# Attention logits: four float32 row tiles of 32 channels instead of stacks of float32r halves

## The chip, the cores and the metric

The kernel runs on one core of one Trainium2 chip. The metric is the device time of one execution in microseconds (us); lower is better. The kernel before takes 4385.15 us, the median of three runs (4384.52 to 4387.54).

## What is computed

Two layers on an image batch x of shape (2, 256, 64, 64), all in float32. A "position" is one of the 4096 pixels of an image.

```python
# layer 0: group norm, then a Mamba block over 4096 positions, residual added
x = x + _L0_conv_ref(_gn(x), ...)
# layer 1: group norm, then attention with 8 heads of 32 channels, residual added
qkv = jnp.einsum('bchw,oc->bohw', x, qkv_w) + qkv_b[None, :, None, None]
q, k, v = ...                                  # (2, 8 heads, 32 channels, 4096)
attn_logits = jnp.einsum('bhci,bhcj->bhij', q, k) * scale
attn_weights = jax.nn.softmax(attn_logits, axis=-1)
out = jnp.einsum('bhij,bhcj->bhci', attn_weights, v)
x = x + out
```

## The kernel before

The program has two stages, one after the other on the same core.

**Mamba stage** (`mamba_stage`, L263). Each image is cut into 8 tiles of 512 positions, 16 tiles in all. One tile's work is 32 steps of the recurrence plus projections before (`front`), gates (`gate`) and the feed-forward part after (`back`). Every operation is handed to a planner with `add(engine, due, cost, emit, reads, writes)`; `Plan.order` (L185) then writes out one fixed order of instructions per engine. It takes, whenever an engine is free in its own bookkeeping, the ready task with the smallest due time, adds `SWITCH` to a task that needs another activation table, and refuses tasks more than `HORIZON` ahead of the oldest one. So the due times, not the program text, set the order in the queues. While image 1 is in this stage, `qkv` (L715) also computes queries, keys and values of image 0: TensorE projects, ScalarE writes the rounded high half in float32r (`high`, L751), VectorE writes the remainder (`low`, L755), and both halves go to DRAM (L760).

**Attention stage** (`attention`, L969). Heads are taken in groups of four (128 channels). A query tile has 512 positions, so there are 2 images x 2 groups x 8 = 32 query tiles. For each, a loop runs over 32 key blocks of 128 positions; one turn of it is called a step here, and there are 1024. A step s does, in the order in which `run` (L1261) issues it:

- `exponentials(s, 0)` and `(s, 1)`: ScalarE reads the logits of two heads (128 x 1024) from PSUM and writes their exponentials to SBUF. The first pair of heads goes into a `chunk` (a tile that collects several terms), the second into a tile `e`.
- `values(s - 1)`: four TensorE matmuls, one per head, 32 output columns each, so that they occupy four column tiles of the array at once. They add into `po`.
- `logits(s + 1, 0)` and `(s + 1, 1)`: two matmuls each. The logits land in tiles `s` of two PSUM banks, of which there are three (`ps_s`, bufs=3). The tiles are used in turn, so the second half of one step takes over the tile that the first half of the step before has filled, and has to wait until that exponential has been read out.
- `add_up(s)`: the softmax denominators. VectorE sums a full chunk with one TENSOR_REDUCE (L1183) and puts the sum as first term into the next chunk. GpSimd and VectorE add up the second pair of heads.

At the start of the next query tile `finish` (L1226) copies `po` out of PSUM (L1232, on VectorE) before the next tile's first `values` may write there, since `po` has one buffer. Later, four more matmuls sum over the partitions (L1242), and reciprocal, scaling and residual follow.

A logit matmul before is one float32r matmul over 128 rows: for each head the rows hold the 32 channels four times, as high and low halves of keys against high and low halves of queries. `load_stack` (L954) builds these stacks from DRAM: a 512-position query tile is read by four DMAs, a key tile of one group by two. Keys of the second group replace those of the first while its last query tile runs (L1271). Between the images `prepare` (L1076) computes image 1's queries, keys and values on the spot (`project`, L1040, `project_values`, L1062): halves go out to DRAM through chunk tiles and the keys come back as stacks.

A chunk before holds four terms, so at steps c = 3, 6, 9, ... 30 of each query tile a reduce of 4 x 1024 elements per partition runs, ten per tile. The last (c = 30) writes `acc_sb`.

Of the kernel before, what the change touches and what calls it, by code (L numbers as in the profile page):

```python
# [23 lines left out]
D = 32  # L24
# [231 lines left out]
SWITCH = 10  # L256
HORIZON = 28
# [5 lines left out]
def mamba_stage(ctx, tc, xs, stats_out, consts, w, outs, scratch):  # L263
# [70 lines left out]
    def first(b, t, due):  # L334
        xt = Buf(r_h)
        load = lambda: nc.sync.dma_start(xt.tile, image_tile(xs[b], t))
        stats = lambda k: nc.vector.bn_stats(stats_in[b][:, k, t, :], xt.tile[:, k, :])
        if b == 0:

            xt.tile = r_h.make()  # L340
            load()
            for k in range(KC):
                stats(k)
            return
        add("SP", due + 8, 0.8, load, [], [xt], lands=3.0)
        for k in range(KC):
            add("DVE", due + 1.5, 0.7, lambda k=k: stats(k), [xt], [stats_bufs[b][k * NT + t]])
# [102 lines left out]
    def group_norm(b, k, due):  # L450
# [27 lines left out]
        add("PE", due, 0.4, lambda: matmul(p1.tile[:, 0:1], [(gmat, s.tile[:, 0:1])]), [s], [p1])  # L478
        add("DVE", due + 1, 0.6, spread, [p1], [s])
        add("PE", due - 1.5, 0.4, lambda: matmul(p2.tile[:, 0:1], [(gmat, s.tile[:, 4:5])]), [s], [p2])  # L480
        add("ACT", due, 0.6, root, [p2], [s, out], ("exp",))
        add("DVE", due - 7.5, 0.2, shift, [s], [out])
# [10 lines left out]
    def front(i):  # L493
# [10 lines left out]
        if i:  # L504
            add("SP", due - 43.5, 1.7, lambda: nc.sync.dma_start(yn.tile, image_tile(xs[b], t)), [], [yn], lands=3.3)
        for k in range(KC):
            add("ACT", due - 31, 0.72, lambda k=k: norm(k), [yn[k], scales_buf[b * KC + k]], [yn[k]])
# [3 lines left out]
        add("PE", due - 40, 1.72, lambda: matmul(mean.tile, [(lnmat, yn.tile[:, k, :]) for k in range(KC)]), [yn], [mean])  # L511
        sq = [Buf(r_tmp) for _ in range(KC)]
        var = Buf(mm)
        for k in range(KC):
# [4 lines left out]
            add("DVE", due - 40.5, 0.6, centre, [mean], [yn[k]])  # L519
            square = lambda k=k: nc.scalar.activation(sq[k].tile, yn.tile[:, k, :], AF.Square)  # L520
            add("ACT", due - 32.5, 0.52, square, [yn[k]], [sq[k], var] if k == 0 else [sq[k]])
# [6 lines left out]
        add("PE", due - 41.5, 1.72, lambda: matmul(var.tile, [(lnmat, s.tile) for s in sq]), sq, [var])  # L528
        add("ACT", due - 36.5, 1.19, rstd, [], [var], ("exp",))
        for k in range(KC):  # L530
# [9 lines left out]
            add("DVE", due - 45, 0.66, scale, [var], [yn[k]])  # L540
            add("ACT", due - 35.5, 0.62, shift, [], [yn[k]])
# [19 lines left out]
        add("PE", due - 11, 3.44, project, d.u, [pp, proj, bc])  # L561
        add("ACT", due - 3, 0.48, lambda: nc.scalar.copy(proj.tile[:NP, :], pp.tile[:NP, :]), [pp], [proj])
        add("ACT", due - 13.5, 0.48, lambda: nc.scalar.copy(bc.tile, pp.tile[:NP, :]), [pp], [bc])
        add("SP", due - 14, 0.4, store_bc, [bc], [d.bc], lands=1.6)
        add("DVE", due - 16, 0.72, halves, [pp, proj], [proj])
# [4 lines left out]
    def conv(d, b, k, due):  # L570
# [13 lines left out]
        add("PE", due - 10, 1.72, project, [d.yn], [px, xm])  # L584
        add("ACT", due - 5, 0.15, lambda: nc.scalar.copy(xm.tile[:, 0:HALO], halo[:, b, k, :]), [h], [xm[0]])
        add("ACT", due + 2, 0.49, lambda: nc.scalar.copy(xm.tile[:, HALO:], px.tile), [px], [xm[1]])
        add("ACT", due + 4, 0.25, lambda: nc.scalar.copy(halo[:, b, k, :], xm.tile[:, T:]), [xm], [h])
        add("PE", due + 4.5, 3.44, convolve, [xm], [pc, d.u[k]])
        add("ACT", due + 0.5, 0.59, silu, [pc], [d.u[k]], ("silu",))

    def softplus(d, k, due):
# [22 lines left out]
        add("PE", due - 3.5, 0.5, lambda: matmul(pd.tile, [(w_dt[:, i, bass.ts(k, P)], d.proj.tile) for i in range(2)]), [d.proj], [pd, dt, lw])  # L614
        add("ACT", due - 2, 1.76, exps, [], [pd, dt], ("exp",))
        add("ACT", due + 2.5, 0.97, logs, [pd], [lw, w1], ("exp",))
        add("DVE", due - 3, 0.58, rest, [pd], [w1])
        add("POOL", due + 7, 1.23, lambda: nc.gpsimd.tensor_sub(lw.tile, lw.tile, w1.tile), [w1], [lw])
        add("POOL", due + 5.5, 1.23, lambda: nc.gpsimd.tensor_add(dt.tile, dt.tile, lw.tile), [lw], [dt])
        add("SP", due + 9, 0.9, lambda: store(d.dt[k], dt, "dt_dram"), [dt], [d.dt[k]], lands=2.0)  # L620
        add("POOL", due - 0.5, 1.23, lambda: nc.gpsimd.tensor_mul(lw.tile, dt.tile, d.u[k].tile), [dt, d.u[k]], [lw])
        add("SP", due + 9.5, 0.9, lambda: store(d.dtu[k], lw, "dtu_dram"), [lw], [d.dtu[k]], lands=2.0)

    def gate(d, k, due):
# [7 lines left out]
        add("PE", due + 7.5, 1.72, project, [d.yn], [pz, z])  # L632
        add("ACT", due + 9, 0.5, lambda: nc.scalar.activation(z.tile, pz.tile, AF.Silu), [pz], [z], ("silu",))

    def back(i):
# [5 lines left out]
        for m in range(KC):  # L641
# [13 lines left out]
            for k in range(0, KD, 2):  # L655
                reads = [yn[m], *d.z] if k == 0 else d.z[k : k + 2]
                work = 2.58 if k == 0 and b == 0 else 1.72
                add("PE", due + 2 * m - 3.5, work, lambda k=k, project=project: (project(k), project(k + 1)), reads, [po])
# [3 lines left out]
            else:  # L662
                plus = lambda m=m, po=po: nc.vector.tensor_add(yn.tile[:, m, :], yn.tile[:, m, :], po.tile)
                add("DVE", due + 2 * m - 1.5, 0.6, plus, [po], [yn[m]])
        hid = Buf(r_hid, KH)
        xt = Buf(r_xb, KC)
        add("SP", due + 5, 1.7, lambda: nc.sync.dma_start(xt.tile, image_tile(xs[b], t)), [], [xt], lands=3.3)
        for f in range(KH):
# [8 lines left out]
            add("PE", due + 5 + 1.5 * f + 0.5, 1.72, up, [yn], [ph, hid if f == 0 else hid[f]])  # L677
            add("ACT", due + 6 + 1.5 * f - 6.5, 0.59, gelu, [ph], [hid[f]], ("gelu",))
        for m in range(KC):
# [12 lines left out]
            for f in range(0, KH, 2):  # L692
                reads = [hid, yn[m], *([xt[m]] if b == 0 else [])] if f == 0 else [hid[f], hid[f + 1]]
                work = 1.72 if f else 3.44 if b == 0 else 2.58
                add("PE", due + 19 + 4 * m + f / 2, work, lambda f=f, down=down: down(f), reads, [acc])
# [11 lines left out]
            if b == 0:  # L707
                add("ACT", due + 24 + 4 * m + 4, 0.59, end, [acc], [xt[m]])
            else:
                add("DVE", due + 24 + 4 * m - 3, 0.76, end, [acc], [xt[m]])  # L710
            add("DVE", due + 25 + 4 * m - 0.5, 0.61, stats, [xt[m]], [stats_bufs[IMAGES + b][m * NT + t]])
        store = lambda: nc.sync.dma_start(image_tile(outs[b], t), xt.tile)
        add("SP", due + 29.5, 1.7, store, [xt], [stored[b * NT + t]], lands=3.3)

    def qkv(b, t, due):  # L715

        hid = Buf(r_hid, KH)
        halves = [hid[5], hid[6]]

# [17 lines left out]
        add("SP", due + 4, 1.7, load, [stored[b * NT + t]], [hid], lands=3.3)  # L737
        for c in range(KC):
            w_parts = [hid[0]] if c == 0 else [hid[1], hid[2]]
            add("SP", due + 1 + c + 7, 1.3, lambda c=c: load_weights(c), [], w_parts, lands=3.0)  # L740
        for k in range(KC):
            add("ACT", due + 3.5, 0.71, lambda k=k: norm(k), [hid[3 + k], scales_buf[(IMAGES + b) * KC + k]], [hid[3 + k]])
        for n, (i, m) in enumerate(((1, 0), (1, 1), (0, 0), (0, 1))):
# [5 lines left out]
            def high(i=i, m=m, pm=pm):  # L749
                bias = b_qkv[:, i * KC + m : i * KC + m + 1]  # L750
                nc.scalar.activation(hid.tile[:, 5, :].bitcast(F32R), pm.tile, AF.Identity, bias=bias)  # L751

            def low(i=i, m=m, pm=pm):
                bias = b_qkv[:, i * KC + m : i * KC + m + 1]
                nc.vector.scalar_tensor_tensor(  # L755
                    hid.tile[:, 6, :].bitcast(F32R), pm.tile, bias, hid.tile[:, 5, :], ALU.add, ALU.subtract
                )

            def store(i=i, m=m):
                nc.sync.dma_start(  # L760
# [730 lines left out]
```

## Time and profile before

The profiled execution took 4385.95 us; its span on the core is 4384.2 us, so 1.75 us lie around the span, and it stands 0.8 us above the median of the runs.

| stretch of the trace | from to (us) | what |
|---|---|---|
| Mamba stage | 0 to 1996 | 16 tiles; 115 to 116 us each for image 0, 117 us each for image 1 |
| attention, image 0 | 1996 to 3137 | 16 query tiles of 70.8 us |
| prepare | 3137 to 3232 | projections of image 1 |
| attention, image 1 | 3232 to 4384 | 16 query tiles of 70.8 us and the end |

The page gives for each engine its busy time, for groups of instructions the number, the mean duration and the idle time before them with its releaser. A matmul's record covers the whole pipeline, so records of TensorE overlap; the distance between the starts of two is the time that one takes of the array. A float32 matmul appears as two records of 512 columns (start to start 0.43 us each where nothing else is in the way, e.g. at L688), a float32r matmul as one.

### The profile page before, as it was taken

What the parts mean: (1) busy time and instruction counts of PE and PEld (TensorE: products, weight loads), DVE (VectorE), ACT (ScalarE), POOL (GpSimd) and SP (SyncE); (2) the same over time, 40 slices, a digit from 0 to 9 for tenths busy, and PEclk for the clock granted to TensorE, in tenths of its full rate; (3) what the DMA queues carried; (4) which work ended last, traced back from release to release, by engine and by line L of the source; (5) the groups of instructions that cost most, each with busy time, mean ns of one, the idle gap of its engine ahead of it and who ended that gap; (6) DMA issues with size and microseconds to landing.
All of it is one profiled execution on the core that took longest, in us unless ns stands there. A gap on an engine that the chain in (4) does not pass through costs nothing.

```text
span 4384.2 us, 53753 instructions
## 1 busy us (share of the span) xinstructions
PE 4208.9 (96%) x18594; PEld 1644.3 (38%) x18594; DVE 3879.8 (88%) x3309; ACT 3765.4 (86%) x4982; POOL 3726.1 (85%) x1913
## 2 busy tenths in 40 slices
PE   6799999999999999989999999999999999999998
PEld 2233333333333433333333333333443333333333
DVE  5899999999999999985888888888758888888898
ACT  5788988988888888767999999999669999999997
POOL 3999999999999999985888888888548888888886
PEclk8899999999999999999999999999999999999999
DMA  6333333333444444436010221010362010410100
GB/s 210 108 109 126 129 117 118 118 125 125 161 166 154 158 157 151 149 115 148 17 27 18 51 70 27 18 27 20 100 196 56 27 27 24 100 27 18 27 20 9
DMA packets 172281, 389.24 MB, mean 89 GB/s; under 512 B 23392, under 2 KB 49760, under 8 KB 163808
## 3 DMA queue, kind: packets, MB, share of 16 engines
q1 hardware_dynamic: 171120, 383.37, 28.5%
q10 hardware_dynamic: 880, 2.36, 0.2%
q8 instruction: 148, 2.42, 0.2%
q14 instruction: 133, 1.09, 0.1%
HBM read 292.33 MB, written 93.32 MB: 88 GB/s over the span
## 4 chain that ended last, share of the span: by engine, by line
PE 80%; DVE 10%; ACT 4%; issue 2%; DMA 2%; POOL 1%; SPq 0%; DVEq 0%; POOLq 0%; ACTq 0%
PE s L1161 26%; PE po L1191 24%; PE mm L448 14%; DVE h L869 6%; PE mm L688 4%; PE y L901 4%; PE bn L448 2%; PE mm L647 2%; DVE bn L860 1%; ACT L248 1%; ACT da L853 1%; PE s L1046 1%; PE y L899 1%; PE sums_ps L1242 1%; DMA dtu_dram<-lw 1%
## 5 line engine op out<-in xcount | busy, mean ns | idle before, releaser
L1183 DVE TENSOR_REDUCE chunk<-chunk 128x1024 f32<-128x4096 f32 x288 | 1270.6, 4412 | 242.2 <-ACT chunk L1174 242.1
L1224 POOL TENSOR_TENSOR acc_p<-acc_p,e 128x1024 f32<-128x1024 f32 x480 | 1151.8, 2400 | 196.8 <-ACT e L1174 178.4
L1174 ACT ACTIVATE chunk<-s 128x1024 f32<-128x1024 f32 x992 | 1121.2, 1130 | 185.7 <-PE s L1161 144.1
L1161 PE MATMUL s<-q,k 128*128 128x512 f32 x4096 | 1227.2, 421 | 7.3 <-ACT chunk L1174 6.4
L875 POOL TENSOR_TENSOR h<-h,c 128x1024 f32<-128x1024 f32 x512 | 1202.7, 2373 | 29.3 <-issue 13.3
L1191 PE MATMUL po<-chunk,v 128*32 128x512 f32 x3968 | 1121.2, 642 | 0.0
L1191 PE MATMUL po<-e,v 128*32 128x512 f32 x4224 | 1079.2, 605 | 0.0
L1174 ACT ACTIVATE e<-s 128x1024 f32<-128x1024 f32 x1056 | 1071.9, 1018 | 7.6 <-PE s L1161 7.2
L1161 PEld LDWEIGHTS s<-q,k 128*128 128x128 f32 x4096 | 690.5, 188 | 1015.6 <-issue 914.8
L853 ACT ACTIVATE da<-dt_rep,neg_a 128x512 f32<-128x512 f32 x1024 | 695.8, 702 | 106.5 <-DVE h L869 103.6
L1222 POOL TENSOR_TENSOR acc_p<-acc_p,e 128x512 f32<-128x512 f32 x480 | 620.4, 1293 | 129.2 <-ACT e L1174 106.6
L869 DVE TENSOR_TENSOR_SCAN h<-da,state,dbu 128x512 f32<-128x512 f32 x512 | 650.8, 1274 | 15.7 <-PE y L901 7.4
L869 DVE TENSOR_TENSOR_SCAN h<-da,state,bn 128x512 f32<-128x512 f32 x512 | 646.3, 1262 | 11.1 <-PE y L901 5.4
L864 POOL TENSOR_TENSOR dbu<-dtu_rep,b 128x1024 f32<-128x1024 f32 x176 | 417.3, 2371 | 19.8 <-issue 7.7
L448 PE MATMUL bn<-proj,pick 112*128 112x512 f32 x512 | 342.7, 671 | 85.6 <-DVE h L869 82.6
L248 ACT ACT_TABLE_LOAD x312 | 400.3, 1283 | 6.3 <-PEq L1481 0.7
L860 DVE TENSOR_TENSOR bn<-dtu_rep,bn 128x512 f32<-128x512 f32 x512 | 346.1, 678 | 18.0 <-DMA dtu_rep<-dtu_dram 9.2
L1221 DVE TENSOR_TENSOR acc<-acc,e 128x512 f32<-128x512 f32 x448 | 310.7, 694 | 30.4 <-ACT e L1174 17.3
L901 PE MATMUL y<-h,sum 128*32 128x512 f32 x2048 | 302.9, 615 | 9.7 <-POOL h L875 9.5
L1191 PEld LDWEIGHTS po<-chunk,v 128*32 128x32 f32 x3968 | 144.1, 108 | 361.4 <-issue 350.5
L448 PE MATMUL mm<-yn,w_in 128*128 128x512 f32 x512 | 256.2, 626 | 8.3 <-ACT yn L538 3.7
L448 PE MATMUL mm<-yn,w 128*128 128x512 f32 x512 | 240.1, 599 | 0.3 <-ACT hid L675 0.3
(149 smaller groups left out, 4077.1 us busy)
## 6 DMA issues: line engine op xcount, KB each, us to landing
dt_rep<-dt_dram SPq DMA_DIRECT2D x128, 512.0 KB, 5.0
dtu_rep<-dtu_dram SPq DMA_DIRECT2D x128, 512.0 KB, 5.5
k<-qk_dram SPq DMA_DIRECT2D x62, 512.0 KB, 7.3
q<-qk_dram SPq DMA_DIRECT2D x124, 256.0 KB, 4.7
b<-bc_dram SPq DMA_DIRECT2D x64, 256.0 KB, 3.1
c<-bc_dram SPq DMA_DIRECT2D x64, 256.0 KB, 4.1
dt_dram<-dt SPq DMA_DIRECT2D x64, 256.0 KB, 2.2
dtu_dram<-lw SPq DMA_DIRECT2D x64, 256.0 KB, 3.5
```

Of the source, the lines that this page charges most:

```text
L248: self.nc.scalar.preload_act_table_set(self.TABLES[task.table])
L448: nc.tensor.matmul(out, lhsT=lhsT, rhs=rhs, start=(i == 0), stop=(i == len(pairs) - 1))
L853: nc.scalar.activation(da[j].tile, dt.tile[:, j, :], AF.Exp, scale=scale)
L869: nc.vector.tensor_tensor_scan(h.tile[:, j, :], da[j].tile, dbu, initial, ALU.mult, ALU.add)
L875: nc.gpsimd.tensor_tensor(h.tile, h.tile, rows_c.tile.unsqueeze(1).to_broadcast([P, 2, T]), ALU.mult)
L901: nc.tensor.matmul(y.tile[j * PQ : (j + 1) * PQ, :], lhsT=sum4, rhs=pair[j // 2].h.tile[:, j % 2, :], start=False, stop=(qd == NQ - 1),)
L1161: nc.tensor.matmul(ps[:, j, :], lhsT=keys[i // NT, kt][:, h, kj : kj + P], rhs=queries[i][:, h, :], start=True, stop=True)
L1174: nc.scalar.activation(e, todo[s].s[half], AF.Exp, scale=SCALE)
L1183: nc.vector.tensor_reduce(out, terms, AX.XY, ALU.add)
L1191: nc.tensor.matmul(tiles[i].po[h * D : (h + 1) * D, :], lhsT=v[:, c, g * P + h * D : g * P + (h + 1) * D], rhs=todo[s].e[h // 2][:, h % 2, :],
L1222: nc.gpsimd.tensor_add(acc_p[:, 1, :], acc_p[:, 1, :], eb[:, 1, :])
L1224: nc.gpsimd.tensor_add(acc_p, acc_p, eb)
```

## The change

1. Queries and keys are stored as plain float32, one tile of 128 channels (`qk_dram` loses its halves; `load_stack`, `high`, `low` go; the order of output channels of the qkv weights is the natural one). A logit matmul is a float32 matmul over the 32 rows of its head, so that the four heads use four row tiles of the array.
2. Chunks hold six terms instead of four: reduces at c = 5, 10, ... 30, six per query tile, each over 6 x 1024 elements. `e` has seven buffers instead of five.
3. One key tile holds both head groups; all eight stay in SBUF for an image. Image 1's are written there by `project` itself and are only stored to DRAM besides. The bias addition in `project` is split between ScalarE and VectorE.
4. In the Mamba stage image 0's queries and keys take one ScalarE instruction and a DMA of one 128 x 512 tile each. The planner gets `SWITCH` 8 instead of 10, `HORIZON` 32 instead of 28, and new due times for nearly all tasks.
5. The fallback for logits out of range (`attention_any_range`, not executed here) is adapted.

The core of the diff:

```diff
-SWITCH = 10
-HORIZON = 28
+SWITCH = 8
+HORIZON = 32
...
-            def high(i=i, m=m, pm=pm):
+            def evict(n=n, i=i, m=m, pm=pm):
                 bias = b_qkv[:, i * KC + m : i * KC + m + 1]
-                nc.scalar.activation(hid.tile[:, 5, :].bitcast(F32R), pm.tile, AF.Identity, bias=bias)
-
-            def low(i=i, m=m, pm=pm):
-                bias = b_qkv[:, i * KC + m : i * KC + m + 1]
-                nc.vector.scalar_tensor_tensor(
-                    hid.tile[:, 6, :].bitcast(F32R), pm.tile, bias, hid.tile[:, 5, :], ALU.add, ALU.subtract
-                )
...
+                nc.scalar.activation(hid.tile[:, 5 + n % 2, :], pm.tile, AF.Identity, bias=bias)
...
-        self.qk = pool.tile([groups, 2, L // T, 2, D, 4, T], F32, name="qk_dram")
+        self.qk = pool.tile([groups, 2, L // T, P, T], F32, name="qk_dram")
...
-    kp = ctx.enter_context(tc.tile_pool(name="l1k", bufs=NT))
-    ep = ctx.enter_context(tc.tile_pool(name="l1e", bufs=5))
+    kp = ctx.enter_context(tc.tile_pool(name="l1k", bufs=NT + 1))
+    ep = ctx.enter_context(tc.tile_pool(name="l1e", bufs=7))
...
-        return ec.tile([P, 2, 2, T, 2], F32, name="chunk")
+        return ec.tile([P, TERMS // 2, 2, T, 2], F32, name="chunk")
...
+    TERMS = 6
...
+        if i:
+            made = images[1].keys[t] = kp.tile([P, KG, T], F32, name="k")
+        else:
+            made = p2.tile([P, KC, T], F32, name="made")
         for m in range(KC):
             bias = b_qkv[:, i * KC + m : i * KC + m + 1]
...
+            if m == 0:
+                nc.scalar.activation(made[:, m, :], pm[:, m, :], AF.Identity, bias=bias)
+            else:
+                nc.vector.tensor_scalar(made[:, m, :], pm[:, m, :], bias, None, ALU.add)
+        nc.sync.dma_start(scratch.qk[KG : 2 * KG, i, t].rearrange("g p t -> p g t"), made)
...
-                q = queries[i] = p2.tile([P, 4, T], F32R, name="q")
-                load_stack(queue, q, scratch.qk[b * KG + g, 0, t], 0)
+                q = queries[i] = p2.tile([P, T], F32, name="q")
+                queue.dma_start(q, scratch.qk[b * KG + g, 0, t])
...
                 h = 2 * half + j
+                rows = slice(h * D, (h + 1) * D)
                 nc.tensor.matmul(
-                    ps[:, j, :], lhsT=keys[i // NT, kt][:, h, kj : kj + P], rhs=queries[i][:, h, :], start=True, stop=True
+                    ps[:, j, :], lhsT=keys[kt][rows, i // NT, kj : kj + P], rhs=queries[i][rows, :], start=True, stop=True
                 )
...
-            return c if c < 4 else 1 + (c - 4) % 3
+            return c if c < TERMS else 1 + (c - TERMS) % (TERMS - 1)
...
-            elif place(c) == 3:
+            elif place(c) == TERMS - 1:
                 todo["chunk"] = chunk()
```

## The prediction

> **What bounds the kernel now.** First the page: its slices show PE at 9 nearly throughout, and its groups say what TensorE and its neighbours pay.
>
> ```profile
> L1183 DVE TENSOR_REDUCE chunk<-chunk 128x1024 f32<-128x4096 f32 x288 | 1270.6, 4412 | 242.2 <-ACT chunk L1174 242.1
> L1174 ACT ACTIVATE chunk<-s 128x1024 f32<-128x1024 f32 x992 | 1121.2, 1130 | 185.7 <-PE s L1161 144.1
> L1161 PE MATMUL s<-q,k 128*128 128x512 f32 x4096 | 1227.2, 421 | 7.3 <-ACT chunk L1174 6.4
> ```
>
> The exponential waits for the logits (144 us in all); the logits wait for almost nothing. TensorE sets the attention stage's pace. Second, busy time by stage (columns: stretch, length, busy time of PE, PEld, DVE, ACT, POOL, clock, DMA share, GB/s): two stretches of four Mamba tiles each (image 0, image 1), then attention.
>
> ```profile
> 528.30:989.80 461.50, 441.92 (x1393) 169.61 (x1392) 444.84 (x485) 415.23 (x718) 458.60 (x221) 1.00 0.38 124
> 1232.70:1700.70 468.00, 459.18 (x1489) 187.05 (x1488) 462.28 (x517) 414.45 (x726) 459.52 (x221) 1.00 0.46 156
> 2040.00:3137.00 1097.00, 1097.00 (x6080) 417.30 (x6072) 960.82 (x558) 1004.08 (x994) 913.05 (x497) 1.00 0.12 31
> ```
>
> Image 0's Mamba tiles are bound by GpSimd (458.6 of 461.5), image 1's by VectorE, GpSimd and TensorE together (all above 98%). Third, the timeline at the end of a query tile (start, length, engine; from steps 30 to 33):
>
> ```profile
> 2991.29 0.76 PEld L1161 LDWEIGHTS s<-q,k 128*128 128x128 f32 x4 [0.90 <-issue]
> 2992.06 1.12 ACT L1174 ACTIVATE chunk<-s 128x1024 f32<-128x1024 f32 x1 [0.15 <-PE s L1161]
> 2992.41 0.11 PEld L1191 LDWEIGHTS po<-chunk,v 128*32 128x32 f32 x2 [0.36 <-issue]
> 2993.06 1.01 ACT L1174 ACTIVATE e<-s 128x1024 f32<-128x1024 f32 x1
> 2993.21 4.42 DVE L1183 TENSOR_REDUCE acc_sb<-chunk 128x1024 f32<-128x4096 f32 x1 [0.57 <-ACT chunk L1174]
> 2993.47 0.76 PEld L1161 LDWEIGHTS s<-q,k 128*128 128x128 f32 x4 [0.90 <-issue]
> ...
> 2997.55 0.69 DVE L1221 TENSOR_TENSOR acc<-acc,e 128x512 f32<-128x512 f32 x1
> ...
> 2998.14 0.68 DVE L1232 COPY po_sb<-po 128x512 f32<-128x512 f32 x1
> ...
> 2998.91 0.11 PEld L1191 LDWEIGHTS po<-chunk,v 128*32 128x32 f32 x2 [0.36 <-DVE po_sb L1232]
> ```
>
> Two things to see. A step takes 2.18 us, 1.12 for the logits and 1.06 for the values. And the last reduce of a tile, an addition and the copy of `po` end at 2998.83, 0.09 before the next tile's values load their weights, which by TensorE's own rhythm (2.187 a step) were due then anyway: this chain has no slack.
>
> [...] The trace has 0.107 us between two loads of 128 columns. [...]
>
> **The change part by part.** *Logits on TensorE.* Read record by record, before: first weight load to first stream 0.124, four streams 0.2345 apart, the last lasting 0.213, drain 0.107; 1.126 in all. After: load exposed 0.124 (128 columns still), two records' worth of streaming 2 x 0.427 at once for four heads, 0.020 stagger, drain 0.107: 1.105. With values at 1.060, TensorE alone needs 2.165 a step (was 2.187). The gain is 0.02[...].
>
> *What this delays.* Before, the first pair of heads was ready 0.77 after the first load (2991.29 to 2992.06). Now all four finish together: the second record of the second head starts at 0.124 + 0.427 + 0.007 = 0.558; from such a start to the ACTIVATE that waits for it the trace has 0.630 (L675, L586 after float32 matmuls). So the exponential starts at 1.188, runs 1.132, and the weight load waiting for its PSUM tile follows 0.051 later: 2.371. The built order of the changed program confirms that wait: the second logit pair of each step waits for the first exponential of the step before. That load is due 0.013 after the step begins. If one step lasts P, the second pair is late by d = 2.358 - P, and the next step lasts 2.165 + d: two consecutive steps last 2.165 and 2.358 in turn, 2.26 on average. (A late second pair doesn't stop the first: at 828.64 two column tiles of L901 start 0.397 after the other two, and all run on.) Behind the waiting load on TensorE stand the next values, and ScalarE waits for both; ScalarE itself, about 2.03 a step when fed, doesn't bind. Per query tile: 32 x 2.165 + 14.5 x 0.193 + 0.86 for the partition sums (as before: 3.05 - 2.19) = 72.9, before 70.76: +2.2.
>
> *Chunks of six.* Ten reduces of 4.41 become six of 6144/0.96 + 0.145 = 6.55: 5 us less VectorE per tile, which it had idle anyway. But the last one stands in the chain without slack. From step 30's start: exponential ends 2.31, reduce starts 0.03 later and ends 8.88; from a reduce's end to the earliest values load 1.25 (as above): 10.13. TensorE arrives there at 4 x 2.165 + 0.386 - 1.06 = 7.99. Stall 2.15 per tile at 30 tile ends (the last of each image has no successor).
>
> *Sum of attention:* 32 x 2.2 + 30 x 2.15 = 70 + 64 = +134.
>
> *Keys in SBUF, prepare.* The DMAs go off SP's queue, but logits never waited for them (7.3 us over all), so nothing. In prepare TensorE is busy 88.9 of 95 us; without the chunk buffers' DMAs and with the evictions split, most of its gaps can go: -6 (0 to -10). The larger `e` ring: nothing, no wait on it shows.
>
> *Mamba stage.* Image 1's tiles lose 4 x 0.73 us of VectorE (L755) each, eight tiles; behind it stands GpSimd at 459.5 of 468, so at most 2.1 of 117 per tile, and TensorE at 459.2; I take 1 per tile: -8. One table load more per tile (16 in the built order, 1.28 each) is on ScalarE with 12% idle: nothing. The new due times can't be costed from the trace; GpSimd's bound leaves image 0 at most 3 in 460 to gain, a worse order could lose some: bounds -20 and +20. End of the kernel: the last reduce is 2 longer: +2.
>
> Sum: 4385.95 + 134 - 8 - 6 + 2 = 4508. The profiled execution is 0.8 above the median, which changes nothing.
>
> **Rivals.** *No slot wait* (the first pair is ready sooner than I think, or the pairs drift apart): 2.165 a step, stall 10.13 - 7.60 = 2.53; a tile 72.7, 30 of them +1.9, the rest -0.6: 4386 + 56 - 12 = 4430. For it: a wait of only 0.1 us decides. Against: each of its terms is read from a record.
> *Row tiles cheaper, the faster side.* If the group lasts e less than 1.105, the exponential also starts e earlier, and P falls to 2.26 - e. The reduce's stall costs a tile 2.2, so from e = 0.15 on the kernel gets faster; with half the passes (e = 0.43) ScalarE would bind at 2.03 and the time were about 4280. Against: the values' groups, the same passes on column tiles, stream their full 2 x 0.427.
> *Weight loads one after the other.* [...]four loads of 0.107 in turn put the last 0.32 later, 2.47 a step, stall 1.4: about +10 a tile, 4700.
> *The exposed load is short* (0.028 as for 32 columns): 2.165 on average with the slot wait, about 4415.
>
> **How the numbers follow.** Slot wait and stall as costed: 0.60 (4470 to 4550 by the uncertainty of 0.04 in P, and of Mamba). No slot wait or short load: 0.20, 4415 to 4440. Cheaper row tiles, faster: 0.10. Serial loads or a worse Mamba order: 0.10. The range leaves out the last two: 4410 to 4560. Within 0.2% (9 us; about what a measurement of this kernel can tell from no change) 0.03, split off the neighbours.
>
> **What would show it.** In the changed profile: steps alternating near 2.17 and 2.36, weight loads of `s` waiting for ACT chunk; each tile's first values load idle some 2 us behind the `po_sb` copy; reduces of 6.55. Logits that stay 0.77 ahead of their exponential, or a reduce under 5, would prove me wrong, as would Mamba tiles off by over 2 us.

## The result and the profile after

The changed kernel takes 4511.18 us (median of four runs, 4507.45 to 4517.59) against 4384.84 for the kernel before on the same chip: a ratio of 1.0290 (95% interval 1.0272 to 1.0307). It is slower, by 126 us; 4508 was forecast. The profiled execution took 4508.83, its span is 4506.9 (before 4384.2). All medians here are of undisturbed executions: two of the six of experiment 8 fell in a slower state with a lower granted clock (5655 and 7040 us, clock 0.69) and are left out.

First, where the 122.7 us between the two spans lie, by the start of the first exponentials of each step (us):

| stretch | before | after | difference | forecast |
|---|---|---|---|---|
| start to the first exponential (Mamba stage) | 1998.1 | 1986.8 | -11.3 | -8 |
| image 0, step 0 to step 511 | 1137.7 | 1212.9 | +75.2 | half of +134 |
| prepare (to image 1's step 0) | 90.2 | 83.9 | -6.3 | -6 |
| image 1, step 0 to step 511 | 1133.6 | 1198.5 | +64.9 | half of +134 |
| end | 24.5 | 24.8 | +0.3 | +2 |

Then the groups of the page of the changed kernel (busy time, mean ns of one, idle time before them and its releaser), the counterparts of the three shown of before and one more:

```profile
L1141 ACT ACTIVATE chunk<-s 128x1024 f32<-128x1024 f32 x992 | 1120.4, 1129 | 325.4 <-PE s L1128 293.3
...
L1128 PE MATMUL s<-q,k 32*128 32x512 f32 x8192 | 1293.6, 645 | 7.3 <-ACT chunk L1141 6.4
L1150 DVE TENSOR_REDUCE chunk<-chunk 128x1024 f32<-128x6144 f32 x160 | 1048.1, 6551 | 251.0 <-ACT chunk L1141 251.0
...
L1158 PE MATMUL po<-chunk,v 128*32 128x512 f32 x3968 | 1128.3, 647 | 64.9 <-DVE po_sb L1199 64.9
```

ScalarE's wait for the logits grew from 144 to 293 us, the reduce takes 6.55, and the values now wait 64.9 us for VectorE's copy of `po`: 2.16 at each of 30 tile ends. The wait on the PSUM tile hardly shows in this view (6.4 us): while the second pair's load waits, the first pair's matmuls run, so TensorE doesn't count as idle. The wait has to be read from the starts. The timeline of two steps (start, length, engine):

```profile
2613.71 0.51 PEld L1128 LDWEIGHTS s<-q,k 32*128 32x128 f32 x8 [0.91 <-PE s L1128]
...
2614.89 1.12 ACT L1141 ACTIVATE chunk<-s 128x1024 f32<-128x1024 f32 x1
...
2614.98 0.11 PEld L1158 LDWEIGHTS po<-chunk,v 128*32 128x32 f32 x2 [0.76 <-issue]
...
2616.03 0.34 PEld L1128 LDWEIGHTS s<-q,k 32*128 32x128 f32 x8 [0.89 <-issue]
...
2617.12 0.11 PEld L1158 LDWEIGHTS po<-chunk,v 128*32 128x32 f32 x2 [0.76 <-issue]
...
2617.20 1.13 ACT L1141 ACTIVATE chunk<-s 128x1024 f32<-128x1024 f32 x1 [0.29 <-PE s L1128]
...
2618.18 0.50 PEld L1128 LDWEIGHTS s<-q,k 32*128 32x128 f32 x8 [0.90 <-PE s L1128]
```

Steps of 2.32 and 2.15 take turns (2613.71, 2616.03, 2618.18), and in the long ones the group's eight weight loads are spread over 0.51 instead of 0.34. Record by record, the second pair's load in the first of these groups starts at 2613.924, 0.05 after the exponential that began at 2612.75 and took 1.12. Over the whole stage the median step is 2.236 (before 2.187). Single steps lie mostly between 2.13 and 2.34; away from the tile ends two in a row average 2.22 to 2.25.

The end of a tile, as shown of before:

```profile
2596.04 6.55 DVE L1150 TENSOR_REDUCE acc_sb<-chunk 128x1024 f32<-128x6144 f32 x1 [0.65 <-ACT chunk L1141]
...
2602.51 0.69 DVE L1188 TENSOR_TENSOR acc<-acc,e 128x512 f32<-128x512 f32 x1
2603.11 0.68 DVE L1199 COPY po_sb<-po 128x512 f32<-128x512 f32 x1
...
2603.84 0.67 PE L1158 MATMUL po<-chunk,v 128*32 128x512 f32 x2 [2.17 <-DVE po_sb L1199]
...
2605.15 2.09 PE L1128 MATMUL s<-q,k 32*128 32x512 f32 x8
```

The same chain, with TensorE standing still for 2.17 before it. The last line was in nobody's forecast: the group of logits after this pause takes 2.02 (its values load at 2607.17) instead of 1.1. The windows view of three stretches of 3.41 us around it (stretch, length, busy times of PE, PEld, DVE, ACT, POOL, granted clock, DMA; the last line is the earliest) says why:

```profile
2604.60:2608.01 3.41, 3.41 (x16) 0.72 (x16) 2.38 (x1) 0.73 (x1) 1.30 (x1) 0.51 0.00 0
2608.01:2611.42 3.41, 3.41 (x32) 0.81 (x24) 0.00 (x0) 2.94 (x4) 2.01 (x1) 1.00 0.00 0
2601.19:2604.60 3.41, 1.24 (x14) 0.16 (x8) 3.41 (x5) 2.18 (x3) 1.49 (x2) 0.99 0.00 0
```

In the stretch from 2601.19 TensorE was busy for 1.24 of 3.41 us; in the next one its granted clock is half, then full again. Such a stretch is called a half-clock window here. Of 30 tile ends 11 have one such window behind them and two have two; those tiles take 76.05 and 77.2 instead of 74.6. That is 11 x 1.45 + 2 x 2.6 = 21 us.

### The profile page after: what moved, and what is told of

It is laid out like the page before. It is cut to its first block, busy times and chain, and to the rows that moved or that the text cites. A ratio compares the mean times of both kernels' runs of the same rounds, so it can differ in the third digit from the quotient of the medians.

```text
span 4506.9 us, 61328 instructions
## 1 busy us (share of the span) xinstructions
PE 4278.3 (95%) x22690; PEld 1390.8 (31%) x22690; DVE 3743.4 (83%) x3133; ACT 3778.7 (84%) x4982; POOL 3724.1 (83%) x1913
## 4 chain that ended last, share of the span: by engine, by line
PE 80%; DVE 9%; issue 4%; ACT 4%; POOL 3%; DMA 1%; SPq 0%; DVEq 0%; POOLq 0%; ACTq 0%
PE s L1128 26%; PE po L1158 23%; PE mm L448 15%; DVE h L858 4%; PE y L890 4%; PE mm L688 3%; PE bn L448 3%; PE mm L647 2%; POOL h L864 2%; PE s L1015 1%; DVE bn L849 1%; ACT L248 1%; ACT chunk L1141 1%; PE y L888 1%; ACT da L842 1%
## 5 line engine op out<-in xcount | busy, mean ns | idle before, releaser
L1128 PE MATMUL s<-q,k 32*128 32x512 f32 x8192 | 1293.6, 645 | 7.3 <-ACT chunk L1141 6.4
L1150 DVE TENSOR_REDUCE chunk<-chunk 128x1024 f32<-128x6144 f32 x160 | 1048.1, 6551 | 251.0 <-ACT chunk L1141 251.0
L1158 PE MATMUL po<-chunk,v 128*32 128x512 f32 x3968 | 1128.3, 647 | 64.9 <-DVE po_sb L1199 64.9
L1158 PE MATMUL po<-e,v 128*32 128x512 f32 x4224 | 1092.0, 611 | 0.0
L1128 PEld LDWEIGHTS s<-q,k 32*128 32x128 f32 x8192 | 435.8, 185 | 933.4 <-issue 714.6
L448 PE MATMUL bn<-proj,pick 112*128 112x512 f32 x512 | 322.2, 641 | 72.8 <-DVE h L858 72.2
L688 PE MATMUL mm<-hid,w 128*128 128x512 f32 x512 | 237.6, 595 | 0.0
```

Of the source, the lines that this page charges most:

```text
L448: nc.tensor.matmul(out, lhsT=lhsT, rhs=rhs, start=(i == 0), stop=(i == len(pairs) - 1))
L1128: nc.tensor.matmul(ps[:, j, :], lhsT=keys[kt][rows, i // NT, kj : kj + P], rhs=queries[i][rows, :], start=True, stop=True)
L1150: nc.vector.tensor_reduce(out, terms, AX.XY, ALU.add)
L1158: nc.tensor.matmul(tiles[i].po[h * D : (h + 1) * D, :], lhsT=v[:, c, g * P + h * D : g * P + (h + 1) * D], rhs=todo[s].e[h // 2][:, h % 2, :],
```

## The experiments

Theory: the added time is (1) a slot wait (logits that wait for their PSUM tile, the slot) in each second step, since the first exponential starts later and frees its PSUM tile later, and (2) the lengthened last reduce of a tile in a chain without slack, to which the trace of after adds (3) half-clock windows that the pause brings. Rivals: the row-tile group itself is slow by turns; the stall or the half clock belongs to the new form of the logits and not to the reduce; in the Mamba stage, the order alone or the dropped work alone. All times are medians; ratios are to the kernel before on the same chip (4386.7 to 4387.7 us in these runs) with their 95% intervals.

**1. Chunks of four in the changed kernel.**

```diff
-    TERMS = 6
+    TERMS = 4
```

> The changed kernel with chunks of four terms again; logits and keys stay as changed. Theory (slot wait in the logits, lengthened last reduce ahead of the po copy): the last reduce of a tile is 4.41 again, so the 2.16 us stall at the 30 tile ends goes (below 0.3 left) and with it the windows at half clock that follow it; steps stay at 2.24 on average in turns of 2.15 and 2.32. 4511 - 30 x 2.1 - about 20 for the half-clock windows = 4428 (4420 to 4450). Rival (the stall comes from the new form of the logits, not from the chunk's size): 4505 to 4515 with the stall in place.

Measured: 4426.06 us, ratio 1.0089 (1.0072 to 1.0106). Tiles take 72.5 throughout, no half-clock window is left at a tile's end, and the values' wait for the copy is 0.9 us in all. What chunks of six cost is 85 us, and it is stall and clock: VectorE's own busy time in reduces is longer here (1412 us against 1258), not shorter.

**2. Chunks of six, but the last reduce behind the copy of `po`.**

```diff
             if c == NC - 2:
                 tile_.acc = p1.tile([P, 3, T], F32, name="acc_sb")
-                sum_chunk(s, tile_.acc[:, 0:2].rearrange("p h t -> p (h t)"))
+                if i == KG * NT - 1:
+                    sum_chunk(s, tile_.acc[:, 0:2].rearrange("p h t -> p (h t)"))
...
             acc = d.acc
+            if i < KG * NT - 1:
+                sum_chunk(i * NC + NC - 2, acc[:, 0:2].rearrange("p h t -> p (h t)"))
...
-            yield 3
+            yield 5
             ps = ps_2.tile([P, T], F32, name="sums_ps", tag="a2")
```

> The changed kernel, but the last reduce of a tile is issued behind the copy of po (all tiles but the last of each image); the partition sums follow two steps later. Theory: VectorE's total work is the same and reduces stay at 6.55, but the copy of po no longer waits: stall at tile ends below 0.3, no half-clock windows there, 4428 (4420 to 4450), as with chunks of four. Rival (VectorE's work or the size of the reduce itself costs, not its place): 4500 or more.

Measured: 4427.54 us, ratio 1.0093 (1.0077 to 1.0110). Two lines of its page:

```profile
L1150 DVE TENSOR_REDUCE chunk<-chunk 128x1024 f32<-128x6144 f32 x160 | 1048.5, 6553 | 212.4 <-ACT chunk L1141 212.4
...
L1158 PE MATMUL po<-chunk,v 128*32 128x512 f32 x3968 | 1117.1, 641 | 0.0
```

The reduce is as long as ever and the wait is gone (64.9 to 0.0). Only its place in VectorE's queue, ahead of the copy, had a price. Tiles take 72.37.

**3. A longer chain in the kernel before.**

```diff
                 tile_.acc = p1.tile([P, 3, T], F32, name="acc_sb")
-                sum_chunk(s, tile_.acc[:, 0:2].rearrange("p h t -> p (h t)"))
+                out = tile_.acc[:, 0:2].rearrange("p h t -> p (h t)")
+                half = todo[s].chunk.rearrange("p q h t k -> p (h t) q k")[:, :, 0:1, :]
+                nc.vector.tensor_reduce(out, half, AX.XY, ALU.add)
+                sum_chunk(s, out)
```

> The kernel before with one VectorE instruction more per query tile: a reduce over half of the last chunk (2048 elements, about 2.28) into acc_sb ahead of the last reduce, which overwrites it. Logits, keys and chunks are as before. Theory (chain of last reduce and copy of po without slack): passes one for one from 0.1 on, a stall of about 2.2 at each of 30 tile ends and half-clock windows after some of them: 4385 + 66 + up to 20 = 4450 to 4472. Rival (there is slack, and the stall in the changed kernel has another cause): 4385 to 4395.

Measured: 4438.15 us, ratio 1.0117 (1.0101 to 1.0134); tiles of 72.44 (70.76 before), no half-clock window (mean clock 0.985, as in the kernel before). Its timeline at a tile's end:

```profile
2576.54 2.28 DVE L1207 TENSOR_REDUCE acc_sb<-chunk 128x1024 f32<-128x2048 f32 x1
...
2578.92 4.42 DVE L1183 TENSOR_REDUCE acc_sb<-chunk 128x1024 f32<-128x4096 f32 x1
...
2583.85 0.68 DVE L1235 COPY po_sb<-po 128x512 f32<-128x512 f32 x1
...
2584.59 0.65 PE L1191 MATMUL po<-chunk,v 128*32 128x512 f32 x2 [1.62 <-DVE po_sb L1235]
```

The stall is 1.68 a tile and not 2.2. The added reduce reads the first two terms only, which have long been there, so it begins in the 0.57 in which VectorE waited for the last exponential: 2.28 - 0.57 = 1.71 is what the chain grew by, and 1.68 of it comes through. So the chain has next to no slack (0.03, about the rounding of the view). The expected size (4450 to 4472) was wrong because of this overlap, and with a pause of 1.60 the clock stays full at the tile ends.

**4. Longer still, to see the clock without row tiles.** Experiment 3 with one more line ahead of the last reduce:

```diff
+                nc.vector.tensor_copy(tile_.acc[:, 2, :], todo[s].e[1][:, 0, :])
                 sum_chunk(s, out)
```

> The kernel before with two more VectorE instructions ahead of the last reduce of a tile: the reduce over the first two terms (2.28, of which 0.57 lies in VectorE's wait for the exponential) and a copy of 512 columns (0.60 in a row) into acc_sb, both overwritten later. The one-instruction kernel showed a TensorE pause of 1.60 at every tile end and no window at half clock. Theory [...]: the pause becomes 2.2, as in the changed kernel, about half of the tile ends show a half-clock window although no row tile runs, and a tile takes 73.05, or about 1.3 more where one follows: 4387 + 30 x 2.28 + 15 x 1.3 = 4475 (4460 to 4490). Rival (half-clock windows come with the row tiles): none at tile ends, 4455.

Measured: 4500.58 us, ratio 1.0260 (1.0242 to 1.0279), above the expected range. TensorE pauses for 2.40 at each tile's end and not 2.2 (the added copy takes 1.08 where 0.60 was taken), and more tile ends than half are hit. Of 30 tile ends 25 have a half-clock window behind them (mean clock 0.975, before 0.985); those tiles take 74.71, the other five 73.23. The windows view of the stretch with one of the pauses (second line) and of the one behind it (first line), columns as above:

```profile
2606.30:2609.70 3.40, 3.40 (x16) 1.36 (x12) 2.04 (x1) 1.42 (x2) 0.96 (x1) 0.50 0.00 0
2602.90:2606.30 3.40, 1.00 (x10) 0.16 (x8) 3.40 (x5) 1.92 (x2) 1.57 (x2) 1.00 0.78 171
```

No row tile runs in this kernel; the half clock comes with the pause, of 2.40 here. More on it below.

**5. The first pair of heads as float32r.** In the changed kernel, keys and queries of heads 0 and 1 are read as float32r, those of 2 and 3 as float32; the trace then has one record for a matmul of the first pair and two for one of the second (6144 weight loads of the logits, 8192 in the changed kernel). It leaves out the low bits of the first pair's keys and queries, and of image 1's keys.

```diff
...
-                nc.tensor.matmul(
-                    ps[:, j, :], lhsT=keys[kt][rows, i // NT, kj : kj + P], rhs=queries[i][rows, :], start=True, stop=True
-                )
+                k, q = keys[kt][rows, i // NT, kj : kj + P], queries[i][rows, :]
+                if half:
+                    k, q = k.bitcast(F32), q.bitcast(F32)
+                nc.tensor.matmul(ps[:, j, :], lhsT=k, rhs=q, start=True, stop=True)
```

> The changed kernel with the first pair of heads as float32r row tiles of 32 channels (one pass; the low bits of these keys and queries are left out of the computation, and those of image 1's keys for all heads); the second pair stays float32. The second pair sets the group's length as before, so TensorE's work is the same; only the first exponential starts earlier. Theory (slot wait): the second pair's PSUM tile is free in time, every step lasts about 2.13 (1.07 + 1.055) instead of 2.236 on average, and the stall at tile ends stays at 2.1 to 2.5: 4511 - 1022 x 0.105 = 4404 (4390 to 4425). Rival (the row-tile group itself is longer by turns, or ScalarE is late for another reason): steps stay at 2.2 or more, 4490 to 4511. If mixed forms can't run side by side, the group grows and it is slower than 4511.

Measured: 4459.79 us, ratio 1.0174 (1.0157 to 1.0191), between the two expectations (4404, and 4490 or more). The steps are 2.113 throughout, as the theory has it, but the stall (pause 2.07) now has half-clock windows behind it at 24 of 30 tile ends, two of them at 21. So the total decides nothing here; the two effects had to be parted.

**6. The same with the late reduce:** the diffs of experiments 2 and 5 together.

> The changed kernel with two edits together: the last reduce of a tile behind the copy of po, and the first pair of heads as float32r row tiles (the low bits of these keys and queries, and of image 1's keys for all heads, are left out). With the first pair alone, steps came to 2.113 in the trace, but the stalls at tile ends brought more windows at half clock, which hid the gain. Theory (slot wait): without the stalls a tile takes 32 x 2.113 + 0.95 = 68.6 against 72.5 with the late reduce alone; 4427.5 - 31 x 3.9 = 4307 (4295 to 4320). Rival (what the float32r pair gains comes from something that the stall at tile ends hid): over 4380.

Measured: 4325.37 us, ratio 0.9860 (0.9842 to 0.9878). Its timeline:

```profile
2611.06 0.31 PEld L1131 LDWEIGHTS s<-q,k 32*128 32x128 f32 x6 [0.89 <-issue]
...
2611.59 1.13 ACT L1142 ACTIVATE chunk<-s 128x1024 f32<-128x1024 f32 x1
...
2612.12 0.12 PEld L1159 LDWEIGHTS po<-chunk,v 128*32 128x32 f32 x2 [0.76 <-issue]
...
2613.17 0.31 PEld L1131 LDWEIGHTS s<-q,k 32*128 32x128 f32 x6 [0.89 <-issue]
```

The group from first load to the next values is 1.06, because the float32 pair in it is as long as before. Only the first exponential begins sooner, 0.53 after the first load instead of 1.18, and no step waits: 2.113 each, tiles of 69.07 against 72.37 in experiment 2. That is 3.3 a tile and 102 us in all; the slot wait is worth most of it, since 0.013 a step (0.4 a tile) comes from the slightly shorter group and values. (The total is 18 us above the expected 4307: the tile is 0.5 longer than expected, at its ends; why, was not followed up.)

**7. The roles of the pairs exchanged, on top of experiment 2:** the first exponential writes the contiguous `e`, the second the chunk.

```diff
-            if half == 0 and s % NC < NC - 1:
+            if half == 1 and s % NC < NC - 1:
...
-            eb = todo[s].e[1]
+            eb = todo[s].e[0]
...
```

> The changed kernel with the last reduce behind the copy of po and with the roles of the two pairs of heads exchanged: the first exponential of a step writes the contiguous tile e for GpSimd (1.01 in the trace), the second writes the chunk for VectorE (1.13). Same sums, same precision. Theory (slot wait): the second pair's PSUM tile is free 0.12 sooner, at 1.17 + 1.01 + 0.05 = 2.23 from the first load instead of 2.35; steps go in turns of 2.126 and 2.23, 2.18 on average instead of 2.236: 4427.5 - 1022 x 0.056 = 4370 (4360 to 4385), at or just below the kernel before. Rival (steps are set by TensorE's group or by ScalarE's sum of both exponentials, which is unchanged): 4425.

Measured: 4408.57 us, ratio 1.0054 (1.0036 to 1.0072): the right direction, a third of the size.

```profile
2613.67 0.44 PEld L1128 LDWEIGHTS s<-q,k 32*128 32x128 f32 x8 [0.92 <-PE s L1128]
...
2614.90 1.02 ACT L1141 ACTIVATE e<-s 128x1024 f32<-128x1024 f32 x1 [0.15 <-PE s L1128]
...
2615.93 0.35 PEld L1128 LDWEIGHTS s<-q,k 32*128 32x128 f32 x8 [0.91 <-issue]
```

The exponential is 0.11 shorter, but starts 1.23 after the first load instead of 1.18. Why it starts later was not shown. The tile is free at 1.23 + 1.02 + 0.05 = 2.30 instead of 2.36, and the shortest step is 2.14 instead of 2.126. Mean (2.14 + 2.30) / 2 = 2.22; the median of the trace is 2.218. Half of what the exchange gained at the exponential's end was lost at its start.

**8. Terms of a chunk one behind the other, on top of experiment 2.**

```diff
-        return ec.tile([P, TERMS // 2, 2, T, 2], F32, name="chunk")
+        return ec.tile([P, TERMS, 2, T], F32, name="chunk")
...
-            terms = todo[s].chunk.rearrange("p q h t k -> p (h t) q k")
-            nc.vector.tensor_reduce(out, terms, AX.XY, ALU.add)
+            terms = todo[s].chunk.rearrange("p k h t -> p (h t) k")
+            nc.vector.tensor_reduce(out, terms, AX.X, ALU.add)
...
```

> The changed kernel with the last reduce behind the copy of po and with the six terms of a chunk one behind the other in SBUF (the exponential writes 1024 contiguous values; the reduce reads terms 4096 bytes apart) instead of in pairs. Same sums, same precision. Theory (slot wait; the first exponential took 1.13 with stride 2 and 1.01 where it writes contiguous values, and no wait comes with it as in the exchange of pairs): PSUM tile free at 1.17 + 1.01 + 0.05 = 2.23 from the first load, steps in turns of 2.126 and 2.23, mean 2.18: a tile of 70.65 instead of 72.37, 4427.5 - 31 x 1.72 = 4374 (4365 to 4390), a little below the kernel before. If the reduce reads far-apart terms slower than 6.55, VectorE may bind: at twice the time (13.1 x 6 = 79 per tile) over 4650. Rival (the length of the first exponential doesn't matter): 4427.

Measured: 4848.77 us, ratio 1.1045 (1.1029 to 1.1061), the bad branch of what was expected.

```profile
L1150 DVE TENSOR_REDUCE chunk<-chunk 128x1024 f32<-128x6144 f32 x160 | 1775.9, 11099 | 30.5 <-ACT chunk L1141 30.5
L1141 ACT ACTIVATE chunk<-s 128x1024 f32<-128x1024 f32 x992 | 1017.5, 1026 | 737.4 <-PE s L1128 468.0
```

The exponential is down to 1.03, but the reduce takes 11.10 instead of 6.55, six of them 66.6 of a tile's 85.4, and VectorE sets the pace. Whether the shorter exponential would help can't be read from this run. The layout in pairs buys the reduce and pays with 0.1 of each exponential.

**9. The second pair's matmuls first, in the changed kernel.**

```diff
-            ps = s_tile()
-            for j in range(2):
-                h = 2 * half + j
+            todo[s].s.append(s_tile())
+            if half == 0:
+                return
+            for h in (2, 3, 0, 1):
...
```

> The changed kernel with the logits' matmuls of a step issued in the order of heads 2, 3, 0, 1: the pair whose PSUM tile comes free late stands first in TensorE's queue. Same work. Theory (the queue is in order, so a wait at its head delays all four row tiles, whereas in the changed kernel the first pair runs on): every step lasts 1.17 + 1.13 + 0.05 = 2.35 instead of 2.15 and 2.32 in turns; a tile 32 x 2.35 + 0.95 plus a stall of about 1.7 (TensorE reaches the tile's end 0.45 later), and with so short a pause no half-clock windows: 77.9 against 75.1 on average, 4511 + 31 x 2.8 = 4597 (4570 to 4620). Rival (in the changed kernel the late pair holds up the first as well, or the order doesn't matter): 4505 to 4520.

Measured: 4614.17 us, ratio 1.0519 (1.0503 to 1.0534).

```profile
2613.06 0.54 PEld L1130 LDWEIGHTS s<-q,k 32*128 32x128 f32 x8 [0.90 <-issue]
...
2614.36 0.11 PEld L1159 LDWEIGHTS po<-chunk,v 128*32 128x32 f32 x2 [0.76 <-issue]
...
2614.48 1.13 ACT L1142 ACTIVATE chunk<-s 128x1024 f32<-128x1024 f32 x1 [0.33 <-PE s L1130]
...
2615.41 0.55 PEld L1130 LDWEIGHTS s<-q,k 32*128 32x128 f32 x8 [0.89 <-issue]
```

Every step now takes 2.356. The number is the expected one; the reason that I gave is not. It isn't the head of the queue that waits: record by record, heads 2 and 3 start at once (2613.06) and it is head 0's load that starts at 2613.303, 0.05 behind the first exponential of the step before. The tiles of PSUM have changed hands with the order: in the built program heads 0 and 1 now use the same tile in every step, and heads 2 and 3 take turns in the other two. So the late pair is the one that the next first exponential needs, so each step's lateness is handed to the next: from the late load 1.18 to the exponential, 1.13, 0.05. In the changed kernel the first exponential doesn't depend on the late pair, and every second step recovers. The remaining 17 us over 4597 are half-clock windows after all: with a pause of 1.98, half of the tile ends have one.

**10. The same order in the kernel before.**

```diff
-            ps = s_tile()
-            for j in range(2):
-                h = 2 * half + j
+            todo[s].s.append(s_tile())
+            if half == 0:
+                return
+            for h in (2, 3, 0, 1):
                 nc.tensor.matmul(
-                    ps[:, j, :], lhsT=keys[i // NT, kt][:, h, kj : kj + P], rhs=queries[i][:, h, :], start=True, stop=True
+                    todo[s].s[h // 2][:, h % 2, :], lhsT=keys[i // NT, kt][:, h, kj : kj + P], rhs=queries[i][:, h, :], start=True, stop=True
                 )
```

> The kernel before with a step's four logit matmuls in the order of heads 2, 3, 0, 1: no row tile, no longer reduce, the same work on every engine; only the first exponential gets its logits last, and the pair whose PSUM tile comes free with that exponential stands first in TensorE's queue. Theory (slot wait: first exponential's start + its length + 0.05 is a floor for the step): the first exponential starts 0.77 + 2 x 0.2345 = 1.24 after the first load, the tile is free at 1.24 + 1.13 + 0.05 = 2.42, and every step lasts 2.42 instead of 2.187: a tile 78.2 instead of 70.76, 4387 + 31 x 7.45 = 4618 (4600 to 4640). Rival (a step takes what the busiest engine's work takes, which is unchanged): 4387.

Measured: 4398.74 us, ratio 1.0028 (1.0016 to 1.0041). A miss. Of the steps, and then of a tile's end:

```profile
2614.01 0.76 PEld L1163 LDWEIGHTS s<-q,k 128*128 128x128 f32 x4 [0.90 <-issue]
...
2615.24 1.13 ACT L1175 ACTIVATE chunk<-s 128x1024 f32<-128x1024 f32 x1 [0.16 <-PE s L1163]
...
2616.19 0.76 PEld L1163 LDWEIGHTS s<-q,k 128*128 128x128 f32 x4 [0.90 <-issue]
```

```profile
2578.56 0.68 DVE L1233 COPY po_sb<-po 128x512 f32<-128x512 f32 x1
...
2579.29 0.11 PEld L1192 LDWEIGHTS po<-chunk,v 128*32 128x32 f32 x2 [0.80 <-DVE po_sb L1233]
```

The first exponential is indeed 1.23 behind the first load, and its tile is free at 2.41, but the load that waits for it is the third of the four here (heads 0 and 1), which comes 0.34 behind the first. It needs a step of 2.41 - 0.34 = 2.07, less than the 2.187 that TensorE takes anyway. So a late exponential costs nothing as such; in these kernels it costs where start + length + 0.05 is more than a step plus the place of the waiting load in its group. In the row tiles that place is 0.014, since the loads of the four start 6 to 7 ns apart where none waits. The 12 us that remain are the other chain: exponential and reduce are 0.47 later, the first values of a tile wait 0.80 instead of 0.36, 0.43 a tile, 30 x 0.43 = 13. This is experiment 3 once more, with the chain moved and not lengthened.

**11. and 12. The Mamba stage, crosswise:** the kernel before with the changed due times, SWITCH and HORIZON, and the changed kernel with those of before. For example:

```diff
-        add("POOL", g - 2.5, 2.32, times_c, [rows_c], [h])
+        add("POOL", g - 1, 2.32, times_c, [rows_c], [h])
```

> The kernel before with the changed kernel's due times, SWITCH and HORIZON in the Mamba stage; attention, keys in halves and the VectorE step of the keys' low halves (four of 0.73 per tile of image 1, due 1.5 behind the high half) as before. Theory: the 11 us that the Mamba stage gained come from VectorE's dropped work in image 1 and from the new order alike; here only the order is new: -3 to -8, 4377 to 4382. Rival (all from the order): 4374. Rival (all from the dropped VectorE work): 4385 or more.

> The changed kernel with the due times, SWITCH and HORIZON of the kernel before in the Mamba stage (the eviction of queries and keys and its store due where the high half's stood). The new due times with the old work were 50 us slower than before. Theory (the 11 us of the Mamba stage come from VectorE's dropped work in image 1 as much as from the order): first exponential at about 1992 instead of 1987, 4516 (4511 to 4522). Rival (all from the dropped work): 4511 or less. Rival (all from the order, which was made for the new work): 4522 or more.

Measured: 4436.65 us, ratio 1.0113 (1.0095 to 1.0131), with the first exponential at 2054.2 (before: 1998.1); and 4550.04 us, ratio 1.0379 (1.0364 to 1.0395), first exponential at 2025.3 (after: 1986.8). Attention tiles are as in the kernel that each comes from. Both mixtures lose, 56 and 38 us up to the first exponential, nearly all while image 1 is in the stage, where `qkv` of image 0 is interleaved; in the first mixture almost half of it comes behind the last step of the recurrence. So the 11 us belong neither to the order nor to the dropped VectorE work alone; either part without the other loses. What they come from within the pair stays open.

## Why the prediction was right

- **Logits on TensorE**, 1.105 a group: measured 1.071 where nothing is late, so 2.126 a step with the values and not 2.165. The row tiles gain more by themselves than I gave them (0.02 predicted, 0.06 measured). That four of them stream at once was an assumption, since none runs before: there the trace has only the values' column tiles, with loads 6 to 7 ns apart. The trace of after has the row tiles' loads 6 to 7 ns apart too, where none waits. A load of 32 rows and 128 columns takes as long (185 ns on average) as one of 128 rows and 128 columns before (188), one of 128 rows and 32 columns 108. About half of the 0.034 between 1.105 and 1.071 is a slip: the terms given for the group before (0.124, three times 0.2345, 0.213, 0.107) add up to 1.148 and not to the 1.126 of the trace. There the last stream starts 0.807 after the first load, so the load is exposed for 0.807 - 3 x 0.2345 = 0.10. In the changed kernel the second record of the first head starts at 0.535, which is 0.108 + 0.427 and not 0.124 + 0.427.
- **What this delays.** Right in mechanism, shown by experiments 6, 7 and 9: exponential at 1.176 (1.188), 1.131 long (1.132), 0.051, tile free at 2.358 (2.371). The waiting load is due 0.014 into its group, so the long step would be 2.344 (2.358). "Two consecutive steps last 2.165 and 2.358 in turn" was 2.15 and 2.32 in the steps shown; by the prediction's own rule only the mean of two is fixed, here (2.126 + 2.344) / 2 = 2.235, and 2.236 was measured. A tile without stall takes 72.4, not 72.9: +52 in all instead of +70, from the mis-sized group.
- **Chunks of six.** Right in mechanism and size: 6.55 a reduce, stall 2.16 (2.15) at 30 ends, shown by experiments 1 to 3. Its sum of 64 is the 64.9 of the page. The estimate 6144/0.96 + 0.145 is the line through two lengths in the trace of before: 0.68 for a reduce of 512 elements (L1258) and 4.41 for one of 4096.
- **What no step had: the clock.** The pause brings 15 half-clock windows at 13 tile ends, +21 us. 52, 65 and 21 make 138 of the 140 measured. That the forecast's 134 came so close is luck: this omission (21) and the oversized slot wait (18) nearly cancel.
- **Prepare** -6 was -6.3. **Mamba** -8 was -11.3 between these two traces. Single traces scatter here: with the Mamba stage untouched, the first exponential comes at 1985.8 to 1991.4 in eight traces of the changed kernel and its variants and at 1994.9 to 2000.0 in four of the kernel before and its variants, means 8.7 apart. So the number fits, but the reason, less VectorE work in image 1, isn't borne out by experiments 11 and 12. **End** +2 was +0.3.
- **The rivals.** No slot wait (4430) and a short exposed load (4415) fall with the steps of the timeline; serial weight loads (4700) with loads 6 to 7 ns apart. The cheaper row tiles were the nearest (a pass is there one of the two records of a float32 matmul, 0.427 each): the group was e = 0.034 below 1.105, where 0.15 would have made the kernel faster.

A version below both times is experiment 6, at the price of half the logits' low bits. Of the variants of the changed kernel in full float32 that were run, none gets below the kernel before: the best, experiment 7, stays 0.5% above it.

## What to carry to other kernels

When work that finished piece by piece is made to finish all at once, look at who waited for the first piece: its reader starts later, and the buffer that it frees comes later, though the producer is no slower. The test that held in these kernels is one sum, reader's start plus its length plus the signal (0.05 here), against the step plus the place of the waiting load in its group. And before an instruction at the end of a loop is lengthened, ask what stands behind it in its queue: here moving it behind one copy was worth 84 us.

## What the hardware showed besides

- **Half clock after a short pause.** In the traces of before and after, every change of the granted clock lies on a grid of 3.413 us, within 0.01 us, and each half-clock stretch fills one window of that grid or several; only the last, at the end of the program, is cut short. At 30 tile ends of after TensorE pauses for 2.15 to 2.18, mostly across the border of two windows. At the 16 ends with at most 1.51 us of the pause in one window, no half-clock window followed; at the 11 with 1.90 or more, one did; of three with 1.59 to 1.61, two had two behind them and one had none. The pause of 1.60 in experiment 3 had none, the 2.40 in experiment 4 had one at 25 ends of 30. So in these kernels it depends on the pause and on where it falls. This is no general threshold: in the Mamba stage of after a window in which TensorE was busy for 2.01 of 3.41 us (157.20 to 160.61) was followed by one at half clock, and one in which it was busy for 1.52 (1587.39 to 1590.80) wasn't.
- **Reduce with a far stride.** 6144 values in pairs take 6.55 us, the same number 4096 bytes apart 11.10 (experiment 8). What makes the difference was not shown; no other layout was run.
- **Row tiles in float32.** Four heads of 32 channels and 512 columns at once take 1.07 from the first weight load to the next group's, and their loads start 6 to 7 ns apart; four float32r matmuls over 128 rows take 1.126.
